# Moving the second gather of a pair, and the row gather's DMA behind its row numbers, in a two-layer graph network

## The chip, the cores and the metric

One core of one Trainium2 chip. The time is that of one execution on the device, in microseconds; lower is better. TensorE (PE in the profile) does the matrix products, VectorE (DVE) and ScalarE (ACT) the elementwise work, GpSimd (POOL) some elementwise work and the indirect DMAs, SyncE (SP) issues the other DMAs. Each of them works off its own queue in the order in which the kernel was written.

## The reference

Inputs are x (16 batches, 1024 nodes, 128 features), a symmetric 0/1 adjacency with ones on the diagonal, a node mask of ones, and the weights of two layers. Each layer is x + gnn(relu(layernorm(x))).

Layer 0 is masked attention with one head of 128: `softmax(q kᵀ)` over the neighbours that adj marks, times v, through an output projection and a relu.

Layer 1 first thins the adjacency out, row after row: a row with more than 10 neighbours loses those whose rank is a multiple of half their number, and each removal also empties the mirrored entry, so that later rows see it:

```python
def step(carry, n):
    row = jnp.take(carry, n, axis=0)
    num = jnp.sum(row.astype(jnp.int32))
    sf = jnp.where(num > T_DIL, (num + K_DIL - 1) // K_DIL, 1)
    rm = row & (jnp.cumsum(row.astype(jnp.int32)) % sf == 0)
    ...
```

Then three graph convolutions (mean over the neighbours left, two weight matrices, rows scaled to length one), each with relu and batch normalisation over all batches and nodes, and a linear layer over the three results.

## The kernel before, in words

The kernel does attention in 16 steps, one per batch. A step has two halves of 512 queries, a half has eight blocks of 128 keys; for each block `scores` gives one product of queries and keys (L714), ScalarE its exponential (L716), VectorE the product with the adjacency (L717). `values` (L730) multiplies what the half before left by v. Each block is three *ticks* long, so a step has 48.

All other work of the attention stage is cut into pieces and put on ticks by hand. `plan` (L769) takes a generator and a list of ticks; `pace` (L834) goes through the plans at every tick, in the order in which they were made, and lets each generator that is due write its next piece. With `later(n, ...)` a small operation is written n ticks after. So the tick lists `AT_...` (L753 to L763) set the order of the instructions in every engine's queue. A tick is no time: an engine reaches its part of a tick when its queue gets there. Ticks above 47 lie in the following step.

The work planned beside attention:

- `project` (L671): layer norm of the next batch (bn_stats on VectorE, L573; moments and the normalisation hn on POOL, L580 to L586 and L592), transposes (L602), then q, k and v. Its first list is that of even steps.
- `load` (L158), `mirrors` and `bound` (L225): the next adjacency, its symmetry, and which rows of it can lose anything at all. `bound` goes back and forth between TensorE (pf, L237 and L238) and VectorE (away, L240).
- `sort` (L243), in odd steps, for the pair of batches i−1 and i: it puts the rows that matter ahead of the others; `pick` and `slot` hold the places.
- `gather` (L288), once for each batch of the pair: the one-hot rows of the places (L295, VectorE), the row numbers from a product with them (pi, L300, and row, L303), an indirect DMA from POOL's queue that fetches 128 rows of the adjacency (L305, 512 KB), a running sum along each row (left, L309), the codes (L312), their transposes (pt, L316), copies of these by ScalarE (turned, L320), a product with the one-hots again (pq, L324), and the results for the solver (L327 to L331).
- `solve` (L334): an iteration that does the row-by-row thinning for four batches at once; `norms_of_x2` and `store` (L742): moments of the first layer's result, and its rows scattered into a sorted order in HBM by POOL (L548).

The PSUM tiles of the attention stage are two for scores, two for values, one for the projection, one for the solver, and two slots named `pd` that `mirror`, `bound`, `sort` and `gather` take in turn (`bank`, L152). A piece that asks for a third slot waits until the last reader of one of the two has run.

After the last step 22 more ticks work off what is left (the *tail*); the remaining pieces of the last gather and the last solve run beside the first convolution, spread over its ticks (`last_of_dilation`, L929). Then come the three convolutions and the scatter of the results.

Of the kernel before, what the change touches and what calls it, by code (L numbers as in the profile page):

```python
# [9 lines left out]
H16 = mybir.dt.float16  # L10
# [5 lines left out]
P = 128  # L16
B, N, D = 16, 1024, 128
NB = N // P
# [13 lines left out]
S = 2 * P  # L32
# [48 lines left out]
class Dilation:  # L81
# [206 lines left out]
    def gather(self, b):  # L288


        nc = self.nc
        used = self.used[:, b:b + 1]
        onehot = self.pool.tile([P, NB, S], H16, name="onehot", bufs=1)
        for k in range(NB):
            nc.vector.tensor_scalar(onehot[:, k, :], self.iota, self.pick[b - b % 2][:, b % 2, k:k + 1], None, op0=OP.is_equal)  # L295
            if k % 2:
                yield
        pi = self.bank([P, 1], F32)
        for k in range(NB):
            nc.tensor.matmul(pi, onehot[:, k, :P], self.node16[:, k:k + 1], start=(k == 0), stop=(k == NB - 1))  # L300
        yield
        row = self.pool.tile([P, 1], I32, name="row")
        nc.vector.tensor_scalar(row, pi, float(b * N), None, op0=OP.add)  # L303
        rows = self.pool.tile([P, N], F32, name="rows", bufs=1)
        nc.gpsimd.indirect_dma_start(out=rows, out_offset=None, in_=self.adj.rearrange("b n m -> (b n) m"),  # L305
                                     in_offset=bass.IndirectOffsetOnAxis(ap=row[:, 0:1], axis=0))
        yield
        left = self.pool.tile([P, N], H16, name="left", bufs=1)
        nc.vector.tensor_tensor_scan(left[:, ::-1], rows[:, ::-1], rows[:, ::-1], 0.0, op0=OP.add, op1=OP.bypass)  # L309
        yield  # L310
        codes = self.pool.tile([P, N], H16, name="codes", bufs=1)
        nc.vector.scalar_tensor_tensor(codes, rows, 1023.0, left, op0=OP.mult, op1=OP.add)  # L312
        yield
        pt = self.bank([P, NB, P], H16)
        for k in range(NB):
            nc.tensor.transpose(pt[:, k, :], codes[:, k * P:(k + 1) * P], self.identh)  # L316
        yield
        turned = self.pool.tile([P, NB, P], H16, name="turned", bufs=1)
        for h in range(2):
            nc.scalar.activation(turned[:, 4 * h:4 * h + 4, :], pt[:, 4 * h:4 * h + 4, :], AF.Copy)  # L320
            yield
        pq = self.bank([P, S], F32)
        for k in range(NB):
            nc.tensor.matmul(pq, turned[:, k, :], onehot[:, k, :], start=(k == 0), stop=(k == NB - 1))  # L324
        yield
        dg = self.pool.tile([P, P], BF, name="dg")
        nc.vector.scalar_tensor_tensor(dg, pq[:, :P], used, self.identf, op0=OP.mult, op1=OP.mult,  # L327
                                       accum_out=self.dcode[:, b:b + 1])
        nc.vector.tensor_scalar(self.own[:, b, :], dg, 512.0, None, op0=OP.is_gt)
        nc.vector.scalar_tensor_tensor(self.code[:, b, :P], pq[:, :P], used, self.up, op0=OP.mult, op1=OP.mult)  # L330
        nc.scalar.activation(self.code[:, b, P:], pq[:, P:], AF.Copy, scale=used)  # L331
        yield
# [176 lines left out]
@with_exitstack  # L509
def gnn_kernel(ctx: ExitStack, tc: tile.TileContext, a, out):  # L510
    nc = tc.nc
    with tc.tile_pool(name="verdict", bufs=1) as vp:
        flag = fast(tc, a, out, vp)
        bad = nc.values_load(flag[0:1, 0:1])
    tc.strict_bb_all_engine_barrier()
    with tc.If(bad > 0):
        general(tc, a, out)
# [3 lines left out]
def fast(ctx: ExitStack, tc: tile.TileContext, a, out, vp):  # L521
# [136 lines left out]
    with ExitStack() as s1:  # L658
# [83 lines left out]
        def store(b):  # L742
            for k in range(NB):
# [7 lines left out]
        every = lambda first, n, by: [first + by * j for j in range(n)]  # L751

        AT_PROJECT = [m + every(m[4] + 4, 4, 1) + every(m[4] + 12, 10, 3)  # L753
                      for m in ([1, 9, 14, 15, 16], [0, 1, 3, 5, 6])]
        AT_LOAD = every(1, 2 * NB, 3)
        AT_BOUND = [[0] + [first + 3 * (j // 2) + j % 2 for j in range(2 * NB)] for first in (9, 3)]
        AT_MIRRORS = ([20, 23, 29, 33, 35, 39, 42, 44], [13, 16, 19, 22, 25, 29, 33, 41])

        AT_SORT = [27, 29, 31, 32, 33, 35, 36]
        AT_GATHER = ([37, 38, 39, 41, 44, 45, 51, 55, 59, 60, 61, 65, 66],  # L760
                     [68, 69, 70, 71, 74, 75, 81, 85, 89, 90, 91, 93, 94])
        AT_NORMS = ([30, 57, 67, 68, 71], [42, 44, 58, 67, 70])
        AT_STORE = every(75, NB, 2)  # L763

# [4 lines left out]
        def plan(gen, start, ticks):  # L769
            agenda.append((gen, [start + t for t in ticks]))  # L770

        def solve_pieces(b0, b1):
            return 9 * ITER + 3 + 13 * (b1 - b0)

        def plan_step(i):
# [13 lines left out]
            if odd:  # L789
                plan(dil.sort(i - 1), start, AT_SORT)  # L790
                for b, ticks in zip((i - 1, i), AT_GATHER):
                    gathering[b] = dil.gather(b)
# [131 lines left out]
    load_x2(2)  # L924


    GATHER_IDLE = {5: 6, 7: 5}

    def last_of_dilation():  # L929

        for part in range(13 - gather_left, 13):
            next(gathering[B - 1])
            for _ in range(1 + GATHER_IDLE.get(part, 0)):
                yield
        yield from dil.solve(LAST, B)
# [185 lines left out]
    with tc.tile_pool(name="ps1", bufs=2, space=PSUM, reuse_waits="tile") as ps:  # L1121
        for _ in H[0][1]:
            clock.tick()
        rest, stores = last_of_dilation(), last_stores()
        checks = dil.verdict(a["nodemask"], vp, recips)
        _advance(checks)

        tick, TICKS1, PIECES1 = 0, 8 * (B - 1), gather_left + sum(GATHER_IDLE.values()) + solve_pieces(LAST, B)
        entering = iter(())
# [795 lines left out]
```

## Time and profile before

| What | us |
|---|---|
| median of three runs (lowest, highest) | 1248.36 (1247.33, 1252.66) |
| the profiled execution's own time | 1192.21 |
| its span, first to last instruction | 1190.4 |
| TensorE busy in the span | 1049.6 (88%) |
| VectorE busy | 860.0 (72%) |
| ScalarE busy | 727.7 (61%) |
| POOL busy | 566.7 (48%) |

The granted clock of TensorE was 0.966 of full speed over the profiled execution. Of the span, attention takes some 760 us (step 0 starts at 19.66, step 15 at 724.07), the convolutions most of the rest. In a group of the profile, L305 is line 305 of the kernel, the names are tiles (written <- read), then come the count, the busy time in all, the mean time of one in ns, and after a second bar the idle time of the engine just ahead of them with what ended it. Step durations are differences of the starts of a step's first score product.

### The profile page before, as it was taken

How to read it: one execution, taken by the hardware profiler on the slowest of the kernel's cores; microseconds unless marked ns; L12 is line 12 of the kernel's file. 1: busy time of each engine (PE TensorE's matmuls, PEld its weight loads, DVE VectorE, ACT ScalarE, POOL GpSimd, SP SyncE). 2: the span in 40 equal slices, each digit the busy share in tenths (PEclk: the TensorE clock that was granted, in tenths of full speed). 3: DMA queues.
4: the chain of work that ended last, by engine and by line, in shares of the span. 5: the costliest groups of instructions: out<-in, count | busy, mean ns of one | idle time of the engine just before them, and what ended most of it. 6: DMA issues, size and time to landing. Idle time of an engine off the chain costs nothing.

```text
span 1190.4 us, 22335 instructions
## 1 busy us (share of the span) xinstructions
PE 1049.6 (88%) x7693; PEld 815.7 (69%) x7723; DVE 860.0 (72%) x2627; ACT 727.7 (61%) x1658; POOL 566.7 (48%) x1063
## 2 busy tenths in 40 slices
PE   7799899899889989989989989878876997999794
PEld 3567677667667666757656657667765997999784
DVE  6767656677777767867867877868887886777742
ACT  5578688677768868767767765246654772333221
POOL 0320743644445346356165270589740101878775
PEclk9999999999999999999999999989899998999897
DMA  6544345344344443543424431243300002788764
GB/s 212 159 130 142 103 129 149 107 127 143 102 121 113 150 124 96 159 124 104 146 87 130 139 104 24 58 109 86 96 1 1 1 1 74 237 246 248 219 195 132
DMA packets 135340, 143.78 MB, mean 121 GB/s; under 512 B 25904, under 2 KB 111280, under 8 KB 135216
## 3 DMA queue, kind: packets, MB, share of 16 engines
q1 hardware_dynamic: 123312, 111.10, 32.5%
q0 software_dynamic: 11904, 31.15, 8.0%
q8 instruction: 63, 1.03, 0.4%
q14 instruction: 61, 0.50, 0.1%
HBM read 113.71 MB, written 28.51 MB: 119 GB/s over the span
## 4 chain that ended last, share of the span: by engine, by line
PE 50%; DVE 22%; POOL 8%; ACT 7%; DMA 6%; issue 5%; POOLq 0%; SPq 0%; DVEq 0%; ACTq 0%
PE ps L714 11%; PE po L730 10%; PE pm L693 6%; PE po L1000 5%; DMA rows<-in_adj_dram,row 4%; DVE e L717 4%; PE pt L1058 2%; DVE left L309 2%; PE ph L1242 2%; ACT e L716 2%; PE pd L193 2%; PE ph L1243 2%; DVE m L366 2%; PE pm L701 2%; POOL out_dram L548 2%
## 5 line engine op out<-in xcount | busy, mean ns | idle before, releaser
L730 PEld LDWEIGHTS po<-vw,e 128*128 128x128 f32 x2048 | 271.8, 193 | 64.9 <-issue 64.5
L730 PE MATMUL po<-vw,e 128*128 128x129 f32 x2048 | 305.6, 283 | 0.0
L714 PE MATMUL ps<-qT,kT 128*128 128x512 f32 x512 | 270.0, 610 | 0.8 <-ACT e L716 0.8
L717 DVE TENSOR_TENSOR e<-e,ab 128x512 f32<-128x512 f32 x256 | 177.4, 694 | 120.7 <-ACT e L716 119.3
L716 ACT ACTIVATE e<-ps 128x512 f32<-128x512 f32 x256 | 152.8, 597 | 102.3 <-PE ps L714 78.5
L548 POOL DMA_INDIRECT x_d<-xt,slot x128 | 143.1, 1118 | 38.3 <-issue 34.9
L167 ACT ACTIVATE ab<-st,d_one_k 128x1024 bf16<-128x1024 f32 x128 | 146.9, 1148 | 1.2 <-DMA st<-in_adj_dram 1.2
L580 POOL TENSOR_SCALAR ln_t<-ln_st 128x8 f32<-128x8 f32 x31 | 7.7, 248 | 289.9 <-DVE ln_st L573 234.6
L184 ACT ACTIVATE junk<-st 128x1024 bf16<-128x1024 f32 x112 | 118.2, 1056 | 0.0
L548 POOL DMA_INDIRECT y_d<-y,nodes x88 | 86.3, 981 | 18.1 <-issue 13.3
L739 ACT ACTIVATE o<-po,recips 128x128 f32<-128x128 f32 x128 | 46.7, 367 | 77.2 <-DVE recips L737 77.2
L1016 ACT ACTIVATE sq<-po 128x512 f32<-128x512 f32 x64 | 38.1, 597 | 78.1 <-PE po L1035 43.5
L714 PEld LDWEIGHTS ps<-qT,kT 128*128 128x128 f32 x512 | 78.4, 192 | 7.5 <-issue 3.1
L592 POOL TENSOR_SCALAR hn<-xt,ln 128x128 f32<-128x128 f32 x120 | 73.8, 626 | 1.6
L309 DVE TENSOR_TENSOR_SCAN left<-rows 128x1024 f16<-128x1024 f32 x16 | 36.6, 2289 | 46.4 <-DMA rows<-in_adj_dram,row 46.4
L199 DVE SCALAR_TENSOR_TENSOR junkv<-pd,ab 128x64 bf16<-128x64 int32 (+7 forms) x128 | 57.6, 450 | 15.1 <-PE pd L193 15.0
L1000 PE MATMUL po<-ws,r 128*128 128x128 f32 x512 | 68.3, 278 | 0.0
L237 PEld LDWEIGHTS <-ab 128*128 128x128 bf16 x448 | 26.4, 97 | 60.7 <-issue 60.1
L592 POOL TENSOR_SCALAR hn<-xt 128x128 f32<-128x128 f32 x112 | 57.0, 518 | 22.7 <-PE pt L602 21.8
L1000 PEld LDWEIGHTS po<-ws,r 128*128 128x128 f32 x512 | 65.6, 195 | 1.1
L1019 DVE TENSOR_REDUCE nrm<-sq 128x4 f32<-128x512 f32 x64 | 43.5, 681 | 22.4 <-ACT sq L1016 22.1
L305 POOL DMA_INDIRECT rows<-in_adj_dram,row x16 | 17.1, 1068 | 83.0 <-DVE row L303 56.5
(330 smaller groups left out, 2414.0 us busy)
## 6 DMA issues: line engine op xcount, KB each, us to landing
st<-in_adj_dram SPq DMA_DIRECT2D x128, 512.0 KB, 3.6
r<-y_d SPq DMA_DIRECT2D x22, 512.0 KB, 5.8
xt<-x_d SPq DMA_DIRECT2D x16, 524.0 KB, 4.0
xt<-in_x_dram SPq DMA_DIRECT2D x16, 512.0 KB, 4.5
x<-x_d SPq DMA_DIRECT2D x16, 512.0 KB, 6.2
out_dram<-r SPq DMA_DIRECT2D x11, 512.0 KB, 4.0
x_d<-xt,slot POOLq DMA_INDIRECT x128, 2.8
y_d<-y,nodes POOLq DMA_INDIRECT x88, 3.5
```

The costliest lines, as they stand in the source:

```text
L167: nc.scalar.activation(ab[:, k, :], st, AF.Exp, bias=self.one_k, scale=ONE_K, accum_out=self.deg[:, b, k:k + 1])
L184: nc.scalar.activation(junk(), st, AF.Exp, scale=-ZERO_K, accum_out=zeros)
L199: nc.vector.scalar_tensor_tensor(junk.rearrange("p a b -> p (a b)")[:, :n], pt.rearrange("p a b -> p (a b)").bitcast(I32)[:, :n], 1.0, ab[ ...
L309: nc.vector.tensor_tensor_scan(left[:, ::-1], rows[:, ::-1], rows[:, ::-1], 0.0, op0=OP.add, op1=OP.bypass)
L548: d = nc.gpsimd.indirect_dma_start(out=dst, out_offset=bass.IndirectOffsetOnAxis(ap=slots, axis=0), in_=src, in_offset=None)
L592: engine.tensor_scalar(hn[:, k, :], xt[:, k, :D], minus[:, k // 2, k % 2, None], rstd[:, k // 2, k % 2, None], op0=OP.add, op1=OP.mult)
L693: nc.tensor.matmul(pp, w, hT[:, 512 * g:512 * g + 512], start=True, stop=True)
L714: nc.tensor.matmul(p, K[b][:, k * P:(k + 1) * P], Q[b][:, c], start=True, stop=True)
L716: later(1, lambda: nc.scalar.activation(e, p, AF.Exp))
L717: later(2, lambda: nc.vector.tensor_mul(e, e, AB_[b][:, k, c]))
L730: nc.tensor.matmul(po[:, q % 2, :], E[k][:, i * P:(i + 1) * P], V[b][:, k, :], start=(k == 0), stop=(k == NB - 1))
L1000: nc.tensor.matmul(po[:, i, :], hT[:, c:c + P], wxk, start=(i == 3), stop=False)
```

## The change

Five edits:

- the one-hot tile of `gather` gets two buffers instead of one;
- `gather` gets one more piece: the indirect DMA is no longer written together with the row numbers but at a tick of its own;
- the codes are written over the running sums, so that the tile codes is gone;
- the tick list of `project` in even steps has its bn_stats and moments (and with them all that follows) two to three ticks sooner;
- the tick lists of both gathers are new. In the first, pi is at 40 (was 44), the row numbers at 41 (was 45), the DMA at 44 (was 45). In the second, the one-hots are at 48, 50, 54, 57 (were 68 to 71), pi at 60 (was 74), the row numbers at 61 and the DMA at 65 (were both at 75). From the scan on both are as they were. As the plan starts with an odd step, 48 is the first tick of the even step after it.

`last_of_dilation` follows: a gather has 14 pieces, and the six idle ticks after the DMA are gone, since in the tail's last tick the DMA has long been written.

```diff
-        onehot = self.pool.tile([P, NB, S], H16, name="onehot", bufs=1)
+        onehot = self.pool.tile([P, NB, S], H16, name="onehot", bufs=2)
...
         nc.vector.tensor_scalar(row, pi, float(b * N), None, op0=OP.add)
+        yield
         rows = self.pool.tile([P, N], F32, name="rows", bufs=1)
...
-        codes = self.pool.tile([P, N], H16, name="codes", bufs=1)
+        codes = left
         nc.vector.scalar_tensor_tensor(codes, rows, 1023.0, left, op0=OP.mult, op1=OP.add)
...
-                      for m in ([1, 9, 14, 15, 16], [0, 1, 3, 5, 6])]
+                      for m in ([1, 7, 11, 12, 13], [0, 1, 3, 5, 6])]
...
-        AT_GATHER = ([37, 38, 39, 41, 44, 45, 51, 55, 59, 60, 61, 65, 66],
-                     [68, 69, 70, 71, 74, 75, 81, 85, 89, 90, 91, 93, 94])
+        AT_GATHER = ([37, 37, 38, 39, 40, 41, 44, 51, 55, 59, 60, 61, 65, 66],
+                     [48, 50, 54, 57, 60, 61, 65, 81, 85, 89, 90, 91, 93, 94])
...
-    GATHER_IDLE = {5: 6, 7: 5}
+    GATHER_IDLE = {8: 5}
...
-        for part in range(13 - gather_left, 13):
+        for part in range(14 - gather_left, 14):
```

## The prediction

> **What bounds the kernel now.** I read the page first, then the windows of each step, then the timeline around one pair of gathers, then TensorE's waits. Page, busy time and two of the groups (busy and mean ns of one, then idle time before them and what ended it):
>
> ```profile
> PE 1049.6 (88%) x7693; PEld 815.7 (69%) x7723; DVE 860.0 (72%) x2627; ACT 727.7 (61%) x1658; POOL 566.7 (48%) x1063
> ...
> L309 DVE TENSOR_TENSOR_SCAN left<-rows 128x1024 f16<-128x1024 f32 x16 | 36.6, 2289 | 46.4 <-DMA rows<-in_adj_dram,row 46.4
> ...
> L305 POOL DMA_INDIRECT rows<-in_adj_dram,row x16 | 17.1, 1068 | 83.0 <-DVE row L303 56.5
> ```
>
> TensorE has most work, but an average over stages says little. One window per attention step (7, 8, 9, 10: length, then busy us of each engine):
>
> ```profile
> 345.21:391.33 46.12, 45.14 (x326) 32.42 (x325) 37.31 (x143) 36.76 (x72) 22.03 (x45) 1.00 0.42 126
> 391.33:437.93 46.60, 41.85 (x293) 29.06 (x292) 29.71 (x85) 33.60 (x66) 22.55 (x45) 1.00 0.40 122
> 437.93:482.26 44.33, 44.02 (x329) 31.71 (x328) 34.24 (x128) 35.88 (x69) 22.52 (x45) 1.00 0.44 136
> 482.26:531.37 49.11, 44.58 (x316) 30.76 (x315) 36.81 (x111) 33.67 (x67) 23.25 (x45) 0.97 0.40 112
> ```
>
> Odd steps (rows 1, 3) are full: TensorE is idle 0.3 to 1.0 us. Even steps idle 4.8 and 4.5 us here; the same subtraction over even steps 2 to 14 gives about 42 us. Only there, in step 0 and in the tail can the change win. Timeline of step 8, three engines:
>
> ```profile
> 411.94 0.15 DVE L303 TENSOR_SCALAR row<-pd 128x1 int32<-128x1 f32 x1
> ...
> 415.80 2.27 POOL L592 TENSOR_SCALAR hn<-xt,ln 128x128 f32<-128x128 f32 x4
> 418.22 1.06 POOL L305 DMA_INDIRECT rows<-in_adj_dram,row  x1 [0.15 <-issue]
> ...
> 422.76 2.29 DVE L309 TENSOR_TENSOR_SCAN left<-rows 128x1024 f16<-128x1024 f32 x1 [6.24 <-DMA rows<-in_adj_dram,row]
> ```
>
> The second gather's row numbers are ready at 411.94; its DMA leaves at 418.22, because POOL first works off two sets of moments and the normalisation, and VectorE then stands 6.24 us in front of the scan. All seven even steps show this (3.8 to 7.4 us), the tail too (4.54 us). The first gather, whose DMA finds POOL idle, waits only twice (2.31 and 0.63 us). What TensorE waits for in steps 2 to 14 (us, times, longest):
>
> ```profile
> PE pd L316 <- DVE codes L312: 9.5, 7, 2.7
> PE pm L693 <- ACT qT L694: 7.1, 5, 1.9
> PE pm L602 <- POOL hn L592: 6.7, 7, 2.3
> PE pd L237 <- DVE d_away L240: 6.7, 9, 1.4
> PE pb L417 <- DVE vw L687: 6.2, 2, 3.2
> PE pb L434 <- DVE low L430: 2.4, 1, 2.4
> ```
>
> Lines 2, 5, 6 (with 1.1 us of smaller ones) follow the stopped scan: 16.8 us, far less than VectorE's 40. Line 1 is at tick 11, the first gather's transposes. Line 3 is tick 31; line 4 ticks 12 and 24.
>
> [...] nothing passes a waiting L316, TensorE stood 1.43 us in step 6. [...] the trace has 4.6 us from POOL's start to landing, once 7.3, and I use that. [...] The trace of before shows no wait for a PSUM slot; I expect one below.
>
> **The change, part by part.** Ticks count from the start of an even step (odd tick minus 48): the second gather's 48 to 65 lie in the even step, whatever the words say. SP issues nothing that is moved; the stores follow the norms on POOL as before.
>
> *Second gather's DMA.* Row numbers move from tick 27 to 13, the DMA from 27 to 17, the scan stays at 33. On POOL it stands behind project's moments (4.8 us from 403.79 in step 8) and ahead of the normalisation. From row numbers near 403.7, it leaves near 408 and lands near 413; the scan comes near 422. Cover 9 us: the stall goes, −16.8. The onehot tile needs its second buffer, since the first gather reads its own until tick 17.
>
> *Normalisation.* Project goes up two or three ticks, so all eight hn (0.6 us each) precede the norms of x2 (4.7 us), which split them in the old order. The DMA's 1.3 us is in front of them, still done about 2 us before the transposes at tick 28: −6.7.
>
> *One-hots off ticks 20 to 23.* Eight instructions, 0.40 us a pair net, 1.6 us of VectorE: the waits at tick 24 (1.14, 0.51, 1.14) go, −2.8.
>
> *One-hots on ticks 0, 2, 6.* Three pairs, 1.2 us, before codes at tick 7. In steps 6, 10, 12, 14 VectorE has no gap there: +1.2 each. Step 2 has 0.39 us of gap (+0.8), step 8 has 1.06 (+0.3), step 4 loses its 2.31 us DMA wait, since the first DMA now leaves at its row numbers four ticks earlier (−1.3). Sum +4.6 on line 1.
>
> *A new wait, at tick 12.* The shared pd tag has two slots. In order: transposes pt at tick 11 (read by ACT at 12 and 13), the second gather's pi now at 12 (read by row at 13), then bound's second pf at 12. It must wait for a reader that is emitted a tick later: row on VectorE or the second turned on ACT. No third-in-line allocation of before precedes such a last read. Behind it on TensorE stand values and all scores. From the end of codes C, the old bound L237 starts at C+1.43 (steps 2, 8), +1.81 (4), +1.92 (10), +1.60 (12), +2.98 (6, 14): 14.1. New: recips come at C+1.24 to 2.84 plus 0.40 for the pair of tick 9; then exp starts 0.46 later, its e product 0.62 after that, row 0.61 after, 0.15 to run, 0.05 to release: 1.89. Sum 28.7; less 14.1, less pi's own 0.2 each (only moved): +13.2. If the slot of pt is taken instead, 0.35 more each, +2.5. I take row, as it is the nearer reader. Lower bound 0, if the slot comes free otherwise; upper 2.5 more.
>
> *First gather, odd step.* Its last pair of one-hots comes at tick 39, pi at 40 instead of 44. Comparing the end of the third pair plus 0.40 with TensorE's place at tick 40: 0.9 us late in pair 6, about 0.8 in pair 14, within 0.1 in the others: +1.8.
>
> *Bn pieces* move within slack of VectorE: between recips and the e product it idles 0.92 us, the two cost 0.70. If that cover is gone, 0.7 a step joins the new wait. *Codes in place*: same instruction, 1.22 us; the next write comes 30 ticks later: 0. *Step 0*: its project waits on POOL anyway (3.19 us at hn), and is now asked for two ticks sooner while its moments start under one tick sooner: +0.5, between −1 and +1.5.
>
> *Tail.* One-hots on its ticks 0, 2, 6 delay the transposes by 1.2 (already 4.51 late). The DMA goes behind six stores and lands near 793 instead of 797.46; the 4.54 us before the scan at 797.48 become about 1, and TensorE's 1.52 and 1.63 us behind it go. Ten fewer ticks of gather start the last solve earlier. Net −3, between −6 and +1.
>
> Sum: −16.8 −6.7 −2.8 +4.6 +13.2 +1.8 +0.5 −3 = −9.2 us against the profiled execution's 1192.2 (1190.4 of span, 1.8 around it). The runs' median is 1248.4, 4.7% more; no view says where. If it is a slower TensorE, the other engines lag less and both sides shrink; I take −7: **1241 us**.
>
> **Rivals.** *A, likeliest:* stall gone, new slot wait pays back half; 1236 to 1245. *B, the slot wait doesn't bite:* 13.2 more, −22, with the slower engine about 1228. For it: before has no slot waits at all, and the releases might come in time; against it, the reader is emitted after the waiter. *C, hidden anyway:* odd steps with no idle show TensorE as the bound; if it runs 5% slower outside the profile, 0.05 us a tick eats the 1 to 3 us waits, and nothing is left: 1248. Against: these waits are real in the profile. *D, slower:* one mechanism, the wait at tick 12. Row or turned comes behind ACT's o, exp and VectorE's queue; −9.2 needs 1.3 us more in each of seven steps to vanish, and 2.2 us more for +6. Steps with solve work (6, 10, 12, 14) could do that if the pieces of tick 11 and 12 get between recips and row: about 1258. Against: recips to exp is 0.46 us in six of the seven steps and 0.80 in the other. That the DMA still comes late is a small part of D: it would need row nine us late.
>
> **How the numbers follow.** A 0.42, B 0.18, C 0.22, D 0.18. 0.5% of 1248 is 6.2 us, about what a measurement tells from no change. A is beyond it in some 0.65 of its cases (0.28), B always: faster 0.46. C and the rest of A: same 0.36. D: slower 0.18. The range holds all of A and C, most of B and the nearer half of D: 1224 to 1258. A's own is 1236 to 1245.
>
> **What would show it.** Right: no scan waits for rows (46.4 us before); hn no longer among TensorE's waits; line 1 about 14 us; L237 in the waits with some 2 us in each of seven even steps, released by row (or turned). Wrong: L237 unchanged (B), the even steps no shorter with their idle moved to tick 12 (C, D), pi in the odd steps with microseconds of wait, or hn still late because the DMA was put ahead of it.

## The result, and the profile after

The changed kernel takes 1248.0 us (median; 1245.1 to 1252.0), the kernel before on the same chips 1252.2 us (1247.3 to 1256.5). The ratio is 0.9972, interval 0.996 to 0.9985: by the ratio some 3.5 us faster, about half of the 7 us that were forecast.

The scans for which the change was made, from the changed kernel's list of groups (busy and mean ns of one, then idle time just before them):

```profile
L310 DVE TENSOR_TENSOR_SCAN left<-rows 128x1024 f16<-128x1024 f32 x16 | 36.5, 2280 | 7.4 <-DMA rows<-in_adj_dram,row 7.4
```

The scans waited 46.4 us for their rows before (43.0 in a second profile of before, see below) and 7.4 us now, all of it once, in the tail. TensorE's waits in steps 2 to 14 of the changed kernel:

```profile
PE pd L317 <- DVE left L313: 13.6, 7, 3.0
PE pm L694 <- ACT kT L695: 10.9, 4, 2.9
PE pd L237 <- DVE row L303: 8.4, 6, 1.4
PE pd L300 <- DVE d_away L240: 4.1, 6, 1.7
...
PE pd L237 <- ACT turned L321: 1.9, 1, 1.9
```

The first line is the transposes at tick 11, at 13.6 us where about 14 was forecast. Lines 3 and 5 are the wait for a pd slot that was forecast for tick 12: bound's product waits for row six times and for turned once. The wait for hn has shrunk to 0.4 us. Line 4, the second gather's product pi waiting at tick 12, belongs to the same place. Only line 2 stands in no forecast.

**Which profile of before to compare with.** The profile that the forecast was made from shows 1192.2 us, and every run beside it some 1250. So before was profiled again, on a chip where it takes 1250.8 us (span 1249.0, clock 0.947). Its TensorE waits in steps 2 to 14 (from L304 on, the changed kernel's line numbers are one higher than before's):

```profile
PE pm L693 <- ACT kT L694: 8.7, 4, 2.9
PE pm L602 <- POOL hn L592: 7.3, 7, 2.3
PE pd L316 <- DVE codes L312: 7.0, 7, 1.8
PE pd L237 <- DVE d_away L240: 6.7, 9, 1.4
PE pb L417 <- DVE vw L687: 6.3, 2, 3.2
PE pm L693 <- ACT qT L694: 5.2, 5, 1.9
```

The wait for kT, in the odd steps, is here without the change (8.7 us), and is absent from the first profile. The list of all waits of this second profile also has a releaser that the first lacks altogether:

```profile
DVE r L1075 <- remote: 28.6, 7, 5.4
```

Idle time that the trace puts down to "remote" comes to 89.3 us in all over VectorE and ScalarE, up to 5.4 us at a time, most of it in the convolutions. On one other chip before takes 1195 us, and no such line is in any profile taken there. The changed kernel was run on it too:

| | before | changed | ratio |
|---|---|---|---|
| chips of the comparison, median us | 1252.2 | 1248.0 | 0.9972 (0.996 to 0.9985) |
| the chip of 1195 us, median us | 1195.3 | 1187.3 | 0.9936 (0.991 to 0.9961) |

On which chip the first profile of before was taken is not on record; its time and its lack of remote waits put it beside the chip of 1195 us. With that there are two pairs of profiles to compare. Stages, in us, as differences of the starts of each step's first score product:

| Stage | first profile of before → changed, chip of 1195 us | second profile of before → changed, chips of 1250 us |
|---|---|---|
| step 0 | 46.4 → 48.6 | 47.4 → 48.9 |
| even steps 2 to 14 | 343.9 → 330.5 | 344.6 → 334.9 |
| odd steps 1 to 13 | 314.1 → 316.7 | 331.6 → 332.8 |
| step 15 to the last values | 57.4 → 61.2 | 57.4 → 61.5 |
| from there to the first batch normalisation | 134.2 → 133.5 | 133.8 → 131.5 |
| span | 1190.4 → 1185.3 | 1249.0 → 1247.5 |

The gain is where it was expected, in the even steps (−13.4 and −9.7), and part of it is given back at both ends of the attention stage. Each column rests on one profile of each kernel. How far such a profile scatters is seen in the experiment on the tail, whose 16 attention steps are written like the changed kernel's and which ran on a chip of the slower kind: 48.1 for step 0, 332.7 for the even steps, 337.7 for the odd ones. So a row of the last column is good to some 1 to 5 us, and the odd steps' +1.2 says nothing.

On the chip of 1195 us, the windows of step 8 of the changed kernel, then of step 0 and of step 15 with the tail (length, then busy us of TensorE, weight loads, VectorE, ScalarE, POOL; the column after POOL is TensorE's granted clock):

```profile
390.12:434.85 44.73, 41.71 (x295) 29.24 (x294) 30.05 (x84) 34.47 (x67) 22.21 (x45) 1.00 0.38 110
...
20.88:69.49 48.61, 41.46 (x210) 24.90 (x209) 32.49 (x80) 32.05 (x57) 9.50 (x22) 0.89 0.53 150
716.76:777.99 61.23, 51.13 (x370) 39.73 (x369) 47.99 (x177) 16.23 (x38) 22.58 (x40) 0.89 0.12 32
```

Step 8 had 4.8 us of idle TensorE and now has 3.0. Over the seven even steps TensorE is busy for 302 us in both kernels and idle for 41.8 us before, 28.1 us now. The timeline around the second gather in step 8 of the same profile:

```profile
401.99 0.15 DVE L303 TENSOR_SCALAR row<-pd 128x1 int32<-128x1 f32 x1
402.20 0.16 PE L237 MATMUL pd<-d_away,ab 128*128 128x2 bf16 x1 [1.42 <-DVE row L303]
...
406.50 1.04 POOL L306 DMA_INDIRECT rows<-in_adj_dram,row  x1 [0.55 <-PE pd L325]
...
407.59 4.49 POOL L593 TENSOR_SCALAR hn<-xt,ln 128x128 f32<-128x128 f32 x8
```

Row numbers 12 us into the step, the DMA 4.5 us after them behind the moments, then all eight hn in one piece: as forecast. Between the first two lines is the price, TensorE's 1.42 us behind row.

### The profile page after: what moved, and what is told of

The parts are those of the page before. It is cut to its first block, busy times and chain, and to the rows that moved or that the text cites. A ratio compares the mean times of both kernels' runs of the same rounds, so it can differ in the third digit from the quotient of the medians.

```text
span 1247.5 us, 22353 instructions
## 1 busy us (share of the span) xinstructions
PE 1079.4 (87%) x7723; PEld 834.2 (67%) x7723; DVE 859.4 (69%) x2627; ACT 730.4 (59%) x1658; POOL 563.7 (45%) x1063
## 4 chain that ended last, share of the span: by engine, by line
PE 60%; DVE 21%; ACT 6%; POOL 5%; another core or an unknown queue 4%; issue 3%; DMA 1%; DVEq 0%; POOLq 0%; ACTq 0%; SPq 0%
PE po L731 14%; PE ps L715 13%; PE pm L694 6%; PE po L1001 5%; DVE e L718 3%; PE pd L193 2%; PE ph L1300 2%; PE pt L1059 2%; POOL hn L593 2%; PE ph L1243 2%; ACT e L717 2%; PE ph L1244 2%; DVE left L310 1%; PE pm L702 1%
## 5 line engine op out<-in xcount | busy, mean ns | idle before, releaser
L731 PEld LDWEIGHTS po<-vw,e 128*128 128x128 f32 x2048 | 279.0, 198 | 66.0 <-issue 65.6
L731 PE MATMUL po<-vw,e 128*128 128x129 f32 x2048 | 315.1, 289 | 0.0
L715 PE MATMUL ps<-qT,kT 128*128 128x512 f32 x512 | 277.2, 625 | 0.8 <-ACT e L717 0.8
L715 PEld LDWEIGHTS ps<-qT,kT 128*128 128x128 f32 x512 | 81.0, 198 | 7.3 <-issue 2.9
L593 POOL TENSOR_SCALAR hn<-xt,ln 128x128 f32<-128x128 f32 x120 | 68.5, 582 | 1.2
L237 PEld LDWEIGHTS <-ab 128*128 128x128 bf16 x448 | 27.2, 99 | 59.8 <-issue 59.6
L1243 PE MATMUL ph<-ws,r 128*128 128x128 f32 x256 | 51.5, 284 | 14.7 <-DVE r L1076 12.4
L1076 DVE TENSOR_TENSOR r<-r,ph 128x512 f32<-128x512 f32 x32 | 21.5, 686 | 53.3 <-remote 23.3
```

What stands on the lines that cost most here:

```text
L593: engine.tensor_scalar(hn[:, k, :], xt[:, k, :D], minus[:, k // 2, k % 2, None], rstd[:, k // 2, k % 2, None], op0=OP.add, op1=OP.mult)
L715: nc.tensor.matmul(p, K[b][:, k * P:(k + 1) * P], Q[b][:, c], start=True, stop=True)
L731: nc.tensor.matmul(po[:, q % 2, :], E[k][:, i * P:(i + 1) * P], V[b][:, k, :], start=(k == 0), stop=(k == NB - 1))
L1243: nc.tensor.matmul(pz[:, i, :], r1[b // 2][:, b % 2, c], wl0, start=True, stop=False)
```

## The experiments

The ratios below are to before on the same chip. The tick lists are those of `AT_GATHER` and `AT_PROJECT`.

### Before once more

No edit.

> The kernel before, profiled once more, since the profiled execution of before (1192 us) lies 4% under all its timed runs. Theory 1 (the long waits of TensorE at tick 36 of odd steps in the profile of after, 10.9 us, are the change's): here they are absent, odd steps idle 0.3 to 1.0 us as in the first profile. Theory 2 (they belong to executions of some 1250 us, whatever the kernel): they are here too, 10 us or more over the odd steps. In both, even steps keep the waits for the second gather (16.8 us) and for hn (6.7 us).

Measured: 1250.8 us; waits and stages are those shown above. The waits of the odd steps (kT 8.7 us, hn L694 4.0) are in before as well, as theory 2 has it, so they are no work of the change.

### The slot wait taken away

```diff
-                       [48, 50, 54, 57, 60, 61, 65, 81, 85, 89, 90, 91, 93, 94])
+                       [48, 50, 54, 57, 62, 63, 65, 81, 85, 89, 90, 91, 93, 94])
```

pi and row of the second gather move two ticks back; the DMA stays at 65.

> The changed kernel with pi and row of the second gather at ticks 62 and 63 instead of 60 and 61, so that bound's second product at tick 60 finds the other PSUM slot free. Theory 1 (the slot wait pays back what the change wins): TensorE's waits for row and turned at tick 12, 10.3 us in the profile of after, go, and the time falls by 8 to 11 us against the changed kernel, to 0.990 of before or less. Rival (those waits are hidden: TensorE catches up in the rest of the step): the waits go and turn up elsewhere in the same even steps, the time moves by under 3 us.

Measured: 0.9881 (0.9854 to 0.9909), 1240.2 us. TensorE's waits in steps 2 to 14:

```profile
PE pd L237 <- DVE d_away L240: 7.1, 13, 1.7
```

L237, bound's product, no longer waits for row or turned (8.4 and 1.9 us in the changed kernel). Part of that wait has moved: for d_away the same product waits 7.1 us instead of 1.2. Still the even steps sum to 326.8 us instead of 334.9. Two ticks' difference in one list are worth 0.9%, about 11 us, as theory 1 had it: on these chips the new slot wait ate three quarters of what the change could have given.

### The preparation in the odd step

```diff
-                       [48, 50, 54, 57, 60, 61, 65, 81, 85, 89, 90, 91, 93, 94])
+                       [42, 43, 44, 46, 49, 50, 56, 81, 85, 89, 90, 91, 93, 94])
```

> The changed kernel with the second gather's one-hots at ticks 42, 43, 44, 46 of the odd step, pi at 49, row at 50, the DMA at 56 right behind the first gather's codes. Theory 1 (VectorE's backlog in the first third of even steps is the bound there; odd steps have room on VectorE): waits at ticks 11 and 12 fall to those of before (7.0 for codes, 2.8 for away), no slot wait, time 5 to 9 us under e1_slot, about 0.982 of before. Rival (VectorE is as full at the end of odd steps; the 1.6 us only start sooner): time within 2 us of e1_slot.

> The kernel with the second gather's preparation in the odd step (one-hots at ticks 42 to 46, row numbers at 50, DMA at 56) once more beside these. Theory 1: 0.971 to 0.977 as before, no half-clock stretch in even steps. Rival (its gain hung on that chip): 0.98 or more.

Measured: 0.9741 (0.9716 to 0.9767), 1222.8 us; on the chip of 1195 us 0.9734 (0.9704 to 0.9764), 1161.7 us. It beats both kernels, and lies 17 us under the slot experiment where theory 1 had said 5 to 9. TensorE's waits in steps 2 to 14, on the first chip:

```profile
PE pd L317 <- DVE left L313: 7.5, 6, 2.0
PE pd L237 <- DVE d_away L240: 5.9, 8, 1.5
```

The slot wait is gone, since pi and row are through before pt is allocated, and the one-hots no longer stand in front of the codes at the start of the step, so that line falls from 13.6 to 7.5. The even steps sum to 309.4 us, with a clock of 1.00 in all seven. On the chip of 1195 us they take 308.0 us, but two of the seven hold a stretch at a clock of 0.50, which the expectation had ruled out.

### Only the bn_stats and moments sooner

Before, with the new list of `project` and nothing else:

```diff
-                      for m in ([1, 9, 14, 15, 16], [0, 1, 3, 5, 6])]
+                      for m in ([1, 7, 11, 12, 13], [0, 1, 3, 5, 6])]
```

> Before with one edit: the project list of even steps goes up two to three ticks, gathers and codes stay as they were. Theory 1 (as in the sum of the prediction, the edit is worth its own wait): TensorE's wait for hn in steps 2 to 14, 7.3 us in the like-for-like profile of before, falls below 2 us, and as the second gather's DMA stands behind hn on POOL it leaves about 2 us sooner in each of seven steps, so that VectorE's waits in front of the scan fall by about 10 of their 40 us; some 8 to 11 us in all, ratio 0.991 to 0.994. Rival (the edit pays only together with the new gather, since hn before the norms merely moves the wait to the scan, which TensorE then shares): hn goes from the waits but the time stays, ratio 0.997 to 1.001.

Measured: 0.9943 (0.9923 to 0.9962), at the edge of what theory 1 said. The wait for hn goes from 7.3 to 0.4 us, and VectorE's wait in front of the scans from 43.0 to 31.5, as it has it. This one list, alone, does no less than the whole change (0.9972) with its five edits. The second gather's DMA, behind hn in POOL's queue, is carried along: it leaves 4.7 us after its row numbers in step 2, where it left 6.3 after them.

### The old project list under the new gather

The kernel of the slot experiment with the old list of `project`:

```diff
-                      for m in ([1, 7, 11, 12, 13], [0, 1, 3, 5, 6])]
+                      for m in ([1, 9, 14, 15, 16], [0, 1, 3, 5, 6])]
```

> e1_slot with the old list of project in even steps (1, 9, 14, 15, 16). Theory 1 (bringing project forward is worth TensorE's wait for hn): the wait for hn, 0.4 us in e1_slot, comes back with 6 to 7 us, and the time rises by 5 to 7 us, to 0.993 of before. Rival (hn's wait is only moved: TensorE waits anyway, or the DMA at tick 65 now lies behind the moments and holds hn up more): the time moves by under 2 us, or rises by more than 9.

Measured: 1.0094 (1.0067 to 1.0122), 27 us slower than with the new list. TensorE's waits in steps 2 to 14 begin with

```profile
PE pm L603 <- POOL hn L593: 19.0, 8, 4.2
```

so the wait that was 7 us in before is 19 us here. Two causes were possible: the DMA between moments and hn, or the list itself.

### The same, with the DMA out of the way

The kernel with the preparation in the odd step, where the DMA stands ahead of the moments on POOL, with the same edit of `project`:

```diff
-                      for m in ([1, 7, 11, 12, 13], [0, 1, 3, 5, 6])]
+                      for m in ([1, 9, 14, 15, 16], [0, 1, 3, 5, 6])]
```

> The kernel with the second gather's one-hots at ticks 42 to 46, row numbers at 50 and DMA at 56 (ratio 0.974), with the old project list. There the DMA, at tick 8 of the even step, stands ahead of the last moments on POOL under either list, and no longer between moments and hn as it does with tick 65. Theory 1 (the 18.4 us wait for hn that the old list gave with the DMA at tick 65 came of the DMA's place between moments and hn): the wait for hn comes back only to some 7 to 10 us, ratio 0.979 to 0.984. Rival (the old list itself is too late once the other waits are gone, wherever the DMA stands): the wait for hn is again 15 to 20 us, ratio 0.99 to 0.996.

Measured: 0.9996 (0.997 to 1.0022). The wait for hn is 17.8 us. The rival is right, and the kernel is slower even than it said. POOL's and VectorE's timelines in step 2, then in step 10:

```profile
136.83 2.28 DVE L310 TENSOR_TENSOR_SCAN left<-rows 128x1024 f16<-128x1024 f32 x1
136.90 3.77 POOL L593 TENSOR_SCALAR hn<-xt,ln 128x128 f32<-128x128 f32 x4
...
518.75 2.28 DVE L310 TENSOR_TENSOR_SCAN left<-rows 128x1024 f16<-128x1024 f32 x1
518.91 2.12 POOL L584 TENSOR_TENSOR ln_t<-ln_t 128x8 f32<-128x8 f32 x1
```

Between the two halves of hn lie the moments of the first layer's result, from 131.59 to 136.91, as in before. New is what runs beside them. The second scan no longer waits for its rows: in steps 2, 4, 8, 10 and 12 it comes 24 to 27 us into the step instead of 31 to 34.5, and so falls on POOL's moments or on the second half of hn. The POOL instruction that meets it ends only with the scan: of the four hn, the one begun at 136.90 takes 2.47 us, the others 0.45; the moments' instruction at 518.91 takes 2.12 us, elsewhere 0.20. These five steps are the ones in which TensorE waits for hn (3.2 to 4.2 us each); in steps 6 and 14 the scan meets neither hn nor moments, and there is no wait. The five instructions take 9.9 us more than usual, and the wait for hn is 10.5 us longer than in before (7.3). In the first profile of before the second scan of each even step meets a store instead, behind hn: the store begun during the scan takes 2.17 to 2.62 us, the median of all of them being 0.98. In the kernel of the section above it is the same five steps: one instruction of hn or of the moments takes 2.1 to 2.5 us in each. With the new list all hn are through before the scan comes.

So it is not the old list by itself, and not the DMA's place, that costs so much: the sooner scan and the late hn meet. The edit of the list is worth 7 us alone, and 27 us (slot experiment) to 32 us (this kernel, by the ratios, from two chips) where the scan comes sooner.

What the old list costs beside TensorE's idle time is seen in two windows. Step 2 of the kernel with the new list, the section on the odd step:

```profile
112.92:155.11 42.19, 41.50 (x294) 29.24 (x293) 28.70 (x79) 34.36 (x68) 22.21 (x45) 1.00 0.40 120
```

and step 2 with the old one:

```profile
112.64:160.07 47.43, 44.06 (x292) 30.64 (x291) 28.75 (x79) 34.09 (x67) 23.97 (x45) 0.93 0.41 122
```

47.43 against 42.19 us is 5.2 us, of which 2.7 are TensorE's idle time and 2.6 are TensorE being busy for longer with the same products, at a clock of 0.93 instead of 1.00.

### One-hots further back only

The slot experiment with its one-hots behind the codes of tick 7:

```diff
-                       [48, 50, 54, 57, 62, 63, 65, 81, 85, 89, 90, 91, 93, 94])
+                       [56, 57, 58, 60, 62, 63, 65, 81, 85, 89, 90, 91, 93, 94])
```

> As e1_slot, and the second gather's one-hots at ticks 56, 57, 58, 60 instead of 48, 50, 54, 57, behind the first gather's codes. Theory 1 (each pair in front of the codes costs 0.4 us of TensorE's wait at tick 11): that wait falls from 13.6 us to 7 to 9, and the time lies 4 to 6 us under e1_slot. Rival (the wait at tick 11 is only shifted to the later one-hots, as pi then waits for them): time within 2 us of e1_slot.

Measured: 0.9885 (0.9856 to 0.9914), the slot experiment's 0.9881 again. TensorE's waits:

```profile
PE pd L237 <- DVE d_away L240: 13.6, 16, 2.4
...
PE pd L317 <- DVE left L313: 6.4, 7, 1.8
```

The wait for the codes is halved (13.6 to 6.4), and what it lost bound has gained (7.1 to 13.6). The time is the rival's, though it is bound's product that waits and not pi. Over the first 11 of the 32 score products of the even steps VectorE is busy for 95.5 of 99.0 us: there it is nearly full, and the order decides who waits.

### The DMA's place in POOL's queue

The slot experiment with the second DMA at tick 75, as late as the old one; its row numbers stay at 63 (the last pair keeps 65):

```diff
-                    plan(gathering[b], start, ticks)
+                    plan(gathering[b], start, [75 if b % 2 and t == 65 and b + 1 < B else t for t in ticks])
```

> e1_slot with the second gather's DMA at tick 75 again (the last pair's stays at 65); its one-hots, product and row numbers stay early. Theory 1 (what the scan waited for is the place of the DMA in POOL's queue, behind the norms of x2): VectorE waits for rows in front of the second scan again, 2 to 5 us each in seven even steps, and the time rises by 5 to 12 us against e1_slot. Rival (row numbers that were late are the cause; with these early the DMA is in time at tick 75 too): no wait for rows, time within 2 us of e1_slot.

Measured: 1.0026 (1.0007 to 1.0046), 17 us slower than the slot experiment, more than theory 1 had said. From the list of groups:

```profile
L310 DVE TENSOR_TENSOR_SCAN left<-rows 128x1024 f16<-128x1024 f32 x16 | 36.6, 2288 | 31.3 <-DMA rows<-in_adj_dram,row 27.4 <-issue 4.0
```

In step 2 the row numbers are there at 125.5 and the DMA leaves at 138.6. It is the place in POOL's queue that stops the scan, not the row numbers; with early row numbers and a late DMA the kernel is no faster than before.

### The first gather as before

The slot experiment with the first gather's old times, row numbers and DMA both at 45:

```diff
-        AT_GATHER = ([37, 37, 38, 39, 40, 41, 44, 51, 55, 59, 60, 61, 65, 66],
+        AT_GATHER = ([37, 38, 39, 41, 44, 45, 45, 51, 55, 59, 60, 61, 65, 66],
```

> e1_slot with the first gather as in before (one-hots 37, 38, 39, 41, pi 44, row 45, DMA 45). Theory 1 (in the first gather little is won or lost: its DMA was waited for twice, 2.9 us in the first profile, and its one-hots come 1.8 us late for pi in two odd steps): time within 3 us of e1_slot, scans wait for rows by 0 to 3 us in all. Rival (pulling it forward costs in the odd steps more than it gives): the time falls by 3 us or more.

Measured: 0.9886 (0.9861 to 0.9911), as with the new list. The first gather's edit is worth nothing that can be measured.

### The tail

```diff
     def last_of_dilation():
 
+        for _ in range(6):
+            yield
         for part in range(14 - gather_left, 14):
...
-        tick, TICKS1, PIECES1 = 0, 8 * (B - 1), gather_left + sum(GATHER_IDLE.values()) + solve_pieces(LAST, B)
+        tick, TICKS1, PIECES1 = 0, 8 * (B - 1), 6 + gather_left + sum(GATHER_IDLE.values()) + solve_pieces(LAST, B)
```

> The changed kernel with six idle pieces ahead of the last scan in the tail, where before had six between DMA and scan. Theory 1 (the changed tail puts the last scan before its rows: VectorE stood 7.36 us there, 4.54 us before): the wait falls to under 2 us and the time by 3 to 6 us. Rival (that stage has slack, or the stores set its end): the wait goes and the time moves by under 1.5 us.

Measured: 0.9964 (0.9947 to 0.998), the changed kernel's 0.9972. The scan no longer waits for its rows. VectorE's timeline ahead of it:

```profile
809.97 0.69 DVE L1022 TENSOR_REDUCE nrm<-sq 128x4 f32<-128x512 f32 x1 [8.29 <-ACT sq L1019]
...
810.88 2.28 DVE L310 TENSOR_TENSOR_SCAN left<-rows 128x1024 f16<-128x1024 f32 x1
```

VectorE now stands 8.29 us for something else, ScalarE's squares in the first convolution. The rival is right: the last scan's wait, 7.36 us in the changed kernel, is worth nothing that can be measured.

### A wait filled with idle products

The changed kernel, with 24 transposes of the one-hot tile in front of the eight of the codes, in even steps; their results are overwritten:

```diff
         pt = self.bank([P, NB, P], H16)
+        for k in range(0 if b % 2 else 3 * NB):
+            nc.tensor.transpose(pt[:, k % NB, :], onehot[:, k % NB, :P], self.identh)
```

> After with one addition: at tick 11 of each even step TensorE first does 24 idle transposes of the first gather's one-hot tile into the slot that the eight transposes of the codes then overwrite. They need nothing that is late, and at the 0.11 us that one of the eight takes there they fill some 1.5 to 2.5 us of a wait for the codes that is 1.9 us in the mean. Theory 1 (a wait costs a second time, [...] in after this happens five times in even steps, each time just behind the waits of ticks 11 and 12): the half-clock stretches in even steps go down from five to at most two, and the kernel is not slower for 168 more transposes but faster, ratio to before 0.992 to 0.996. Rival (the clock follows something else, and a wait costs its own length only): as many half-clock stretches as before, the work added is partly in addition to the wait, ratio 0.998 to 1.003.

> The changed kernel with the 24 idle transposes at tick 11 of even steps once more, to be compared with the changed kernel on the same chip. Theory 1 (filling the wait keeps the clock up): 0.2% or more below the ratio of the changed kernel, and fewer half-clock stretches in even steps than the five of after. Rival (the 0.9938 of its first run was the chip's): the same ratio as the changed kernel or above it.

> The changed kernel once more, beside the two below and on one chip with them. Before ran at 1250 us on most chips and at 1195 us on one, so a ratio from one chip may not hold on another. Theory 1 (the change's worth does not depend on the chip): 0.995 to 0.9985 again, whatever before takes here. Rival (where before runs at 1195 us the waits of the odd steps are missing and the even steps weigh more): 0.990 to 0.994, near the forecast of 0.994.

Measured, all on the chip of 1195 us: filled 0.9938 (0.9921 to 0.9956) and 0.9943 (0.9918 to 0.9967), the changed kernel itself 0.9936 (0.991 to 0.9961). The first figure alone would have spoken for theory 1; beside the changed kernel on the same chip there is no gain. The wait for the codes fell from 13.6 to 4.5 us, and the time stayed. In the changed kernel three of the seven even steps show a clock under 1.00 (0.90, 0.96, 0.97), in the filled one two (0.93, 0.97) and three (0.93, 0.97, 0.97). In the even steps of the second filled run TensorE is busy for 311.2 us instead of 302.4 and idle for 20.2 instead of 28.1: the filler replaced wait by work. That the waits of tick 11 cost the changed kernel a second time through the clock is not confirmed. What these runs did show is the changed kernel's ratio on another chip, 0.994 as forecast and as the rival of the third expectation had it.

## Where the prediction held and where it failed

Each term in us, beside what TensorE's lines of waits show for it, on the chip of 1195 us and on the chips of 1250 us:

| Step of the prediction | forecast | 1195 us | 1250 us |
|---|---|---|---|
| second gather's DMA, stall behind the scan (qT, vw, low and smaller) | −16.8 | −16.8 | −13.8 |
| hn ahead of the norms | −6.7 | −6.3 | −6.9 |
| one-hots ahead of codes, tick 11 | +4.6 | +4.1 | +6.6 |
| slot wait at tick 12, less tick 24 (+13.2 − 2.8) | +10.4 | +9.6 | +8.9 |
| first gather's pi | +1.8 | +0.5 | 0 |
| step 0 | +0.5 | +2.2 | +1.5 |
| tail | −3 | +3.2 | +1.8 |
| sum | −9.2 | −3.5 | −1.9 |

The fourth row adds the four lines of L237 and L300 behind row, turned and d_away (8.5, 1.6, 2.3, 3.9; on the other chips 8.4, 1.9, 1.2, 4.1) and takes away the 6.7 of before; the 2.3 lies in odd steps. Step 0 and the tail come from the table of stages. The sums are smaller than what was measured (−8.0 and −3.5 us), so the lines of waits do not hold all that the even steps gained.

**Right: what happens in the even steps.** The stall and the wait for hn go, a wait for a slot takes their place, row releases it in six steps and turned in one, line 1 comes to about 14. Rival B is out, since the slot wait bites. So is C: its figure of 1248 is what was measured, but by another way, for waits taken from even steps did shorten them. So is D, since the wait is no larger than forecast. The experiments put a price on the two largest terms from the other side: the slot wait 11 us, the DMA's place 17 us. One reading was a little off: the trace of before does have waits for a pd slot, 0.5 us of `mirror` behind d_code and junkv. The transfer was about as long as the 4.6 us of the forecast: from POOL's start to the scan it was 4.5 us in step 8 of before. What mattered was the DMA's place in POOL's queue: it left 6.3 us after its row numbers there, 13 us after them in an experiment.

**The step that failed: the two ends of attention.** By the table of stages, steps 1 to 14 gained 10.8 us on the chip of 1195 us and 8.5 on the others, more than the 6.7 that the first five rows forecast. Step 0 and the tail were to gain 2.5 together and lost 5.4 and 3.3 us. On the chip of 1195 us the two errors, 4.1 us better and 7.9 us worse than forecast, work against each other, and that its ratio came out at the forecast's 0.994 is luck in part. On the chips of 1250 us the error at the ends, 5.8 us, is larger than all that is missing there (3.5 of 7).

*The tail* was to win 3 us, since the DMA would land 4.5 us sooner and the last scan would wait less. The changed kernel's timeline on the chips of 1250 us:

```profile
803.65 1.00 POOL L306 DMA_INDIRECT rows<-in_adj_dram,row  x1 [0.30 <-issue]
...
808.00 2.29 DVE L310 TENSOR_TENSOR_SCAN left<-rows 128x1024 f16<-128x1024 f32 x1 [7.36 <-DMA rows<-in_adj_dram,row]
```

The DMA went behind six stores as the step said, but it left 66.6 us after the start of step 15 where before (second profile) had 68.7: 2 us sooner, not 4.5. Without the six idle ticks in between, VectorE was ready for the scan at 800.64, ahead of the DMA, and its wait grew from 2.0 to 7.36 us (from 4.54 to 8.20 beside the chip of 1195 us). The experiment on the tail shows that this wait costs nothing that can be measured: the step counted as gain a wait that holds up nothing. And it left out what did change, the stage ahead of it, from step 15 to the last values. Of before, the windows of step 0 and of step 15 with the tail:

```profile
19.66:66.09 46.43, 38.20 (x207) 22.41 (x207) 32.50 (x80) 31.33 (x56) 9.84 (x22) 0.96 0.60 176
724.07:781.42 57.35, 48.06 (x363) 37.32 (x362) 46.29 (x168) 17.03 (x39) 22.23 (x40) 0.95 0.12 33
```

Against the windows of the changed kernel shown above, step 15 with the tail is 3.9 us longer, 3.1 of them busy TensorE, not idle, at a clock of 0.89 instead of 0.95 (by an estimate, (1 − clock) times length, 6.7 us lost instead of 2.9). The clock is not all of it: with a clock of 0.94 this stage takes 57.4 us in before (second profile), 58.4 with the project list alone, and 59.5 in the slot experiment. So, by the slot experiment, some 2 of the 4 us come with the new lists at an equal clock; the rest goes with the lower clock, and why that fell is not settled.

*Step 0* took 1.5 to 2.2 us more where 0.5 was forecast. It is written alike in every kernel with the new project list, and there its clock is anything from 0.86 to 0.93 and its length 48.0 to 49.2 us; with the old list it takes 46.4 to 47.4 us. At the same clock of 0.93 it is 46.8 and 46.9 us with the old list under a new gather, and 48.0 to 48.1 with the new list (four profiles). The list itself thus costs some 1.1 us there, and the rest goes with the clock, which differs between profiles of the same order of instructions.

**Wrong as well: "I take −7".** The step carried −9.2 from an execution of 1192 us to runs of 1248 by supposing a slower TensorE, with smaller waits and smaller gains. But the even steps take 343.9 us in the first profile of before and 344.6 in the second. Of the 58.6 us between the two, 17.5 lie in the odd steps and 37.8 behind the last values of attention, so the even steps had nothing to shrink by. On the chip of 1195 us, beside which the first profile belongs by its time and its lack of remote waits, −8.0 us came out (0.9936 against the forecast 0.994); on the others it was −3.5. Whether the change is really worth more on the one than on the others is not shown: the even steps gain 13.4 us there, 9.7 on the others, and 11.9 with the tail experiment's profile in place of the changed kernel's; the two intervals touch at 0.996; and the variant with the odd-step preparation gains the same 2.6% on both.

## What to carry to other kernels

Before a piece is moved earlier, list the allocations of its rotating tag in program order: if the third of them comes before the last reader of the first, a slot wait is written into the order, and moving by two ticks can be worth more than the move itself (11 us against 3.5 here). A wait's length in the profile is not its worth: the wait for hn was 7 us in the profile, and the edit against it was worth 7 us alone and 27 to 32 us in kernels in which the scan came sooner. When a wait goes, look at what the instruction behind it, now sooner, will run beside. A wait that holds up nothing is no gain when it goes, however long it is: the last scan's 7.36 us. And where an execution's profile and the timed runs differ by 4%, look first at what else differs between the two, before a sum is scaled.

## What the runs showed of the hardware

- **TensorE's granted clock was 0.50 for some stretches of the even steps.** In step 10 of the changed kernel, on the chips of 1250 us, the window ahead of such a stretch and the stretch itself:

```profile
497.40:500.90 3.50, 1.56 (x14) 1.20 (x13) 3.50 (x8) 1.98 (x5) 0.00 (x0) 1.00 0.36 135
500.90:507.70 6.80, 5.51 (x30) 3.71 (x28) 5.32 (x22) 3.32 (x7) 3.03 (x9) 0.50 0.15 57
```

  TensorE was busy for 1.56 of 3.50 us, the other 1.94 being its wait for the codes, and then had a clock of 0.50 for 6.8 us. The even steps of this profile hold five such stretches (steps 4, 6, 10, 12 and 14), those of the first profile of before three (steps 4, 10 and 12), 3.4 us long each but for the 6.8 shown. In the 3.4 us ahead of each of the eight TensorE was idle for 1.6 to 2.5 us. In the two kernels with the odd-step preparation that differ in the list of `project` alone (profiled on two chips of the slower kind), all seven even steps have a clock of 1.00 in one, and 0.93 in six and 0.96 in the seventh in the other. In the filled kernel the wait for the codes fell from 13.6 to 4.5 us and still two and three even steps had a clock under 1.00, so what sets the clock is not shown.
- **One chip was faster.** The medians of before are 1252 to 1255 us in all sets of runs but the two on one chip, where they are 1195 us. The slower ones show waits released by "remote", 89.3 us in all in one profile and up to 5.4 us each; on the chip of 1195 us there are none. What "remote" stands for is not shown, nor that it is the cause.
- **POOL instructions that met VectorE's scan mostly ended with it or within 0.8 us of its end.** In the kernel with the odd-step preparation and the old project list, five POOL instructions of the even steps that run into the 2.28 us scan take 2.12 to 2.47 us, where the same instructions take 0.20 and 0.45 us elsewhere; they end with the scan or 0.26 us after it. In the first profile of before the seven stores begun during the second scan of an even step take 2.17 to 2.62 us and end 0.77 or 0.78 us after it. Two memsets that fall into the last scan of the changed kernel (0.53 and 0.12 us) are not lengthened; the instruction behind them takes 1.67 us, where the median of its line (L899) is 0.24, and ends 0.03 us after the scan. What holds the others up, no run here shows.
- **The single buffer of rows held back a DMA whose row numbers were ready 5.3 us sooner.** In the variant with the odd-step preparation the DMA of step 8 left only when the first gather's codes had been read out of the tile rows:

```profile
394.55 1.22 DVE L313 SCALAR_TENSOR_TENSOR left<-rows,left 128x1024 f16<-128x1024 f32 x1
...
396.04 1.49 POOL L306 DMA_INDIRECT rows<-in_adj_dram,row  x1 [13.69 <-DVE left L313]
```

  Its row numbers had been ready at 390.78. Anything earlier would need a second buffer of 512 KB, which was not tried.
